# Row statistics of a layer norm taken from a router column and from ScalarE instead of VectorE

## The chip, the cores and the metric

The kernel runs on one core of a Trainium2 chip, as one launch. Its metric is the device time of that launch in microseconds (us). Three runs of the kernel before took 476.71, 476.83 and 477.4 us; the median is 476.83. A core has five engines with instruction lists of their own: TensorE (PE for matmuls, PEld for its weight loads), VectorE (DVE), ScalarE (ACT), GpSimd (POOL) and SyncE (SP, here only a queue that issues DMAs).

## The reference

The input x has 4096 tokens of 256 numbers. Two sublayers follow each other, each with a residual and a layer norm over the 256 numbers of a token:

```python
x = layernorm(x + mamba(x))        # y @ W_out is the last product of mamba; y has 512 numbers per token
x = layernorm(x + moe(x))          # each token goes to the one expert of 8 with the largest router logit

def layernorm(x, eps=1e-5):
    m = mean(x);  v = var(x)
    return (x - m) / sqrt(v + eps)
```

The mamba part is: a projection x @ W_in (256 to 1024 columns), a causal convolution over four tokens with SiLU, a small projection to one step size and 2 x 16 state numbers, a recurrence over the tokens with 16 states, a gate, and y @ W_out. The router's logits are `x1 @ Wr.T + br`, x1 being the output of the first layer norm. An expert is 256 to 1024 with ReLU and back to 256. Everything is float32.

## The kernel before, in words

The tokens go in eight blocks of 512 (NB = 8, TB = 512), and a block is four tiles of 128 tokens (JT = 4). The main loop (line 1047) runs eight rounds. Round k does the input projection of block k (`project`, eight column groups of 128), the small projection and the recurrence of block k-1 (`gauge`, `gauge_out`, `scan`), the gate, the output projection and the first layer norm of block k-2 (`gate`, `project_out`, `choose`), and the sorting of the tokens of block k-3 into lists by expert (`rank`, `place`, `blocks_of`, `tokens_of`). After some rounds blocks of 128 tokens of one expert are already sure, and quarters of their expert work (`expert`) are put between the pieces; most of it follows after the loop.

PE's order is the order in which the code is written (`manual_schedule` for PE, line 120). For DVE, ACT and POOL a scheduler orders the instructions when the kernel is built, from its own estimates and the order of the code; at run time each engine works through its list in that order. PSUM has eight banks: three for `mm` (products of `project` and of the experts), three for `o` (`gate`, `project_out`, the experts' second product) and two for `tr` (all else). A matmul into a bank waits until the bank's last reader is done.

The router is folded into the output projection. A layer norm subtracts the mean and divides by the standard deviation, so the logits are `(x + y W_out) @ Wr.T` with the mean taken out, times the inverse deviation, plus `br`. To that end `router_weights` (line 470) takes the mean over the 256 inputs out of the router's weights `wr`; `router_behind` (line 484) multiplies W_out by `wr` and puts the eight columns beside W_out, so `wout` is 256 + 8 columns wide; `look` (line 886) multiplies a block of x by `wr` (32 columns, of which eight are used), and `look_out` (line 901) turns this round, adds its two halves and writes the eight numbers of each token beside the token's x in `xb`, which is 256 + 8 wide as well.

`project_out(i, j)` (line 916) then multiplies tile j of the gated y (`sg`) by `wout` into a bank of 264 columns, and DVE adds that to `xb` (line 924): columns 0 to 255 hold x + y W_out, columns 256 to 263 the raw logits. DVE takes the row statistics with `bn_stats` (line 928) and `bn_aggr` (line 929). After the fourth tile ACT takes the square root of the four variances (line 934), DVE the reciprocal `sd` (line 935) and `nm`, minus mean times `sd` (line 937), and ACT writes the normed rows x1 (line 940), which SP's queue stores to `x1d` in DRAM (line 944). `choose` scales the raw logits with `sd`, adds `br` and picks the expert.

Other lines named below: ACT copies the products of `project` out of PSUM (lines 759, 761 and 763) and applies SiLU (line 772); DVE adds the convolution's taps (line 723); `gauge_out` makes the step sizes with an exponential on ACT (line 816) and a chain of small DVE steps; `scan` takes an exponential on ACT for `dA` (line 848), and on DVE `dBx` (line 850), the recurrence (line 852) and `hC` (line 860); `gate` sums `hC` over the states with a matmul into `py` (line 872), and DVE (line 879) and POOL or DVE (line 884) make `sg`. ACT loads a table of functions (rows named ACT_TABLE_LOAD) where the next function is not in the loaded one.

Of the kernel before, what the change touches and what calls it, by code (L numbers as in the profile page):

```python
# [37 lines left out]
F32 = mybir.dt.float32  # L38
# [3 lines left out]
AF = mybir.ActivationFunctionType  # L42
ALU = mybir.AluOpType
# [4 lines left out]
P = 128  # L48
T, D = 4096, 256
DI, NS, KC = 512, 16, 4  # L50
NE, FF = 8, 1024
TB = 512
NB = T // TB
JT = TB // P
NT = T // P
DC = D // P
CC = DI // P
# [26 lines left out]
OFF = 2 * NE * T  # L84
XW = 2 * NS + 1

O2 = DC * FF
OB = O2 + FC * D
OC = OB + FC
# [10 lines left out]
def mamba_moe(  # L100
# [17 lines left out]
    nc = tc.nc  # L118

    ctx.enter_context(tc.manual_schedule(engines={mybir.EngineType.PE}))  # L120
    const = ctx.enter_context(tc.tile_pool(name="const", bufs=1))
# [3 lines left out]
    a2 = ctx.enter_context(tc.tile_pool(name="a2", bufs=2))  # L125
    a3 = ctx.enter_context(tc.tile_pool(name="a3", bufs=3))

    def bank(tag, name, bufs=None):
        return ps.tile([P, 512], F32, tag=tag, name=name, bufs=bufs)
# [5 lines left out]
    st = {}  # L135

    def load(i):

        xTb = a2.tile([P, DC, TB], F32, tag="xTb", name=f"xTb{i}")
        at = slice(i * TB, (i + 1) * TB)  # L140
        if i:
            nc.sync.dma_start(xTb, xT[:, at].rearrange("(c p) t -> p c t", p=P))

        xb = a2.tile([P, JT, D + NE], F32, tag="xb", name=f"xb{i}")
        st[i] = {"xTb": xTb, "xb": xb}

    def load_rows(i):
        nc.sync.dma_start(
            st[i]["xb"][:, :, 0:D], x[i * TB : (i + 1) * TB, :].rearrange("(j p) d -> p j d", p=P)
        )  # L150

    load(0)


# [18 lines left out]

    wr = const.tile([P, DC, Q], F32, name="wr")
    nc.vector.memset(wr, 0.0)
    nc.sync.dma_start(wr[:, :, 0:NE], WrT.rearrange("(c p) e -> p c e", p=P))
    wx = const.tile([P, CC, H], F32, name="wx")
    nc.vector.memset(wx, 0.0)
    al = const.tile([NS, 1], F32, name="al")
    dp = const.tile([P, CC], F32, name="dp")  # L180

    wout = const.tile([P, CC, D + NE], F32, name="wout")
    brb = const.tile([P, NE], F32, name="brb")
    nega = const.tile([NS, 1], F32, name="nega")

# [10 lines left out]
    eps = const.tile([P, 1], F32, name="eps")  # L196
# [271 lines left out]
    woutT = held_weights[-1][:, 0 : DC * DI].rearrange("p (c n) -> p c n", c=DC)  # L468
# [14 lines left out]

    def router_behind(half):
        po = bank("tr", f"pwo{half}", 2)
        pov = po[:, 0 : CC * NE].rearrange("p (c e) -> p c e", e=NE)
        cs = slice(half * CC // 2, (half + 1) * CC // 2)
        for c in range(CC)[cs]:
            for dc in range(DC):
                nc.tensor.matmul(  # L490
                    pov[:, c, :], lhsT=woutT[:, dc, c * P : (c + 1) * P], rhs=wr[:, dc, 0:NE],
                    start=(dc == 0), stop=(dc == DC - 1),
                )
        nc.scalar.copy(wout[:, cs, D : D + NE], pov[:, cs, :])


    xgs, wes, turned, hid, last, open_, ys = {}, {}, {}, {}, {}, {}, {}
# [104 lines left out]
    def close(b, half):  # L602
# [5 lines left out]
        def out_weights(fc):  # L608
            return we[:, O2 + fc * D : O2 + (fc + 1) * D]

# [290 lines left out]
    def look_out(i):  # L901

        pf = bank("tr", f"pf{i}", 2)
        for s in range(2):
            at = slice(s * P, (s + 1) * P)
            nc.tensor.transpose(pf[:, at], st[i]["rx"][:, at], ident)

        pfv = pf[:, 0 : 2 * P].rearrange("p (s c h e) -> p s c h e", s=2, c=DC, h=2)
        beside = st[i]["xb"][:, :, D : D + NE].rearrange("p (h s) e -> p h s e", s=2)
        parts = a2.tile([P, 2, DC, 2, NE], F32, tag="rparts", name=f"rparts{i}", bufs=1)  # L910
        for s in range(2):
            nc.scalar.copy(parts[:, s], pfv[:, s, :, :, 0:NE])
        turned_parts = parts.rearrange("p s c h e -> p c h s e")
        nc.vector.tensor_tensor(beside, turned_parts[:, 0], turned_parts[:, 1], ALU.add)

    def project_out(i, j):
        s_, sg, xb = st[i], st[i]["sg"], st[i]["xb"]
        po = bank("o", f"po{i}_{j}")
        for c in range(CC):
            nc.tensor.matmul(  # L920
                po[:, 0 : D + NE], lhsT=sg[:, c, j * P : (j + 1) * P], rhs=wout[:, c, :],
                start=(c == 0), stop=(c == CC - 1),
            )
        nc.vector.tensor_tensor(xb[:, j, :], po[:, 0 : D + NE], xb[:, j, :], ALU.add)
        if j == 0:
            s_["mv"] = a2.tile([P, JT, 2], F32, tag="mva", name=f"mva{i}")
        sta = a2.tile([P, 6], F32, tag="sta", name=f"sta{i}_{j}")
        nc.vector.bn_stats(sta, xb[:, j, 0:D])
        nc.vector.bn_aggr(s_["mv"][:, j, :], sta)
        if j < JT - 1:  # L930
            return
        mv = s_["mv"]
        sd = s_["sd"] = a2.tile([P, JT], F32, tag="sda", name=f"sda{i}")
        nc.scalar.activation(sd, mv[:, :, 1], AF.Sqrt, bias=eps)
        nc.vector.reciprocal(sd, sd)
        nm = a2.tile([P, JT], F32, tag="nma", name=f"nma{i}")
        nc.vector.scalar_tensor_tensor(nm, mv[:, :, 0], -1.0, sd, ALU.mult, ALU.mult)
        x1 = a2.tile([P, JT, D], F32, tag="x1", name=f"x1{i}", bufs=1)
        for j in range(JT):
            nc.scalar.activation(  # L940
                x1[:, j, :], xb[:, j, 0:D], AF.Identity,
                scale=sd[:, j : j + 1], bias=nm[:, j : j + 1],
            )
        nc.sync.dma_start(
            x1d[i * TB : (i + 1) * TB, :].rearrange("(j p) d -> p j d", p=P), x1
        )
# [100 lines left out]
    for k in range(NB):  # L1047
        if have(k + 1):
            load(k + 1)
# [5 lines left out]
        a, b, c = k - 1, k - 2, k - 3  # L1055
# [3 lines left out]
        if k == 2:  # L1059
            router_behind(1)  # L1060
# [18 lines left out]
        if have(b):  # L1079
            project_out(b, 0)  # L1080
        expert(fill[3])
        project(k, 4)
        if k == 1:
            router_behind(0)
        if have(c):
            rank(c)
        if have(b):
            project_out(b, 1)
# [5 lines left out]
        if have(b):  # L1094
            project_out(b, 2)
        expert(fill[5])
        project(k, 6)
        if have(a):
            look_out(a)
            scan(a)  # L1100
# [11 lines left out]
    a, b, c = NB - 1, NB - 2, NB - 3  # L1112
# [12 lines left out]
    project_out(b, 2)  # L1125
    expert()
    look_out(a)
    scan(a)
    expert()
# [77 lines left out]
```

## Time and profile before

| | |
|---|---|
| runs, median | 476.71, 476.83, 477.4; 476.83 us |
| profiled execution: time, span | 479.7 us, 478.0 us |
| mean granted TensorE clock | 0.993 |
| PE busy | 466.2 us (98%) |
| DVE busy | 340.4 us (71%) |
| ACT busy | 223.4 us (47%) |
| POOL busy | 185.5 us (39%) |

The profile is of one execution; its span runs from the first to the last instruction, and 1.7 us of its time lie outside. Busy time leaves out waiting. Matmuls are pipelined and their ends are modelled, so a busy PE is not a PE at its peak. A group line gives line, engine, operation, result and operands with shapes, count, busy time, mean time of one, and after the second bar the idle time just before them with what ended it. A line of waits gives engine and line, what it waited for, the total, the number of times and the longest, in us.

### The profile page before, as it was taken

Reading aid. Unit: us, or ns where it says so; the run is one execution under the profiler, and the core shown is the slowest. Engines: PE = TensorE matmul, PEld = TensorE weight load, DVE = VectorE, ACT = ScalarE, POOL = GpSimd, SP = SyncE. Lnnn points to the kernel's source line nnn. Section 1 sums busy time; section 2 is a strip of 40 time slices with the busy share of each in tenths; the row PEclk is TensorE's granted clock in tenths of the full one; section 3 lists DMA queues with packets and bytes.
Section 4 is the critical chain, followed back from the end, with each engine's and each line's share of the span. In section 5 each row is a group of like instructions: output and inputs, shape, how many; then the busy total and the mean of one; then the engine's idle time right before and its main releaser. Section 6 shows DMA issues by size and latency. Waiting matters only on the chain. (4 is left out here: it accounts for less than half of the span.)

```text
span 478.0 us, 7559 instructions
## 1 busy us (share of the span) xinstructions
PE 466.2 (98%) x2606; PEld 350.1 (73%) x2606; DVE 340.4 (71%) x1120; ACT 223.4 (47%) x453; POOL 185.5 (39%) x194
## 2 busy tenths in 40 slices
PE   8999999999999999999999999999999999999994
PEld 6444554645455566677788999999989898989884
DVE  1687959899898997986998978755446565645453
ACT  3776767886896877584625131212212121212111
POOL 2001203442418372450433423435445456654541
PEclk9998999999999999999999999999999999999998
DMA  8401012040124945250766759799997279977910
GB/s 237 166 1 45 0 42 91 1 132 0 47 87 149 431 159 188 110 199 18 271 242 225 270 209 366 260 368 350 359 347 277 60 253 345 313 247 245 353 44 22
DMA packets 23401, 89.98 MB, mean 188 GB/s; under 512 B 4914, under 2 KB 14909, under 8 KB 19650
## 3 DMA queue, kind: packets, MB, share of 16 engines
q0 software_dynamic: 8752, 74.71, 42.7%
q1 hardware_dynamic: 13650, 14.50, 9.3%
q8 instruction: 21, 0.34, 0.3%
q10 hardware_dynamic: 960, 0.27, 0.3%
q14 instruction: 18, 0.15, 0.1%
HBM read 87.78 MB, written 9.43 MB: 203 GB/s over the span
## 5 line engine op out<-in xcount | busy, mean ns | idle before, releaser
L744 PE MATMUL pm<-xTb,win 128*128 128x512 f32 (+1 forms) x264 | 122.5, 598 | 0.0
L587 PEld LDWEIGHTS ph<-xgT,we 128*128 128x128 f32 x864 | 100.8, 192 | 5.5 <-DVE r L637 1.3
L587 PE MATMUL ph<-xgT,we 128*128 128x128 f32 x864 | 103.0, 276 | 0.0
L612 PE MATMUL pe<-we,hT 128*128 128x256 f32 x432 | 98.9, 380 | 0.0
L612 PEld LDWEIGHTS pe<-we,hT 128*128 128x128 f32 x432 | 79.7, 190 | 10.0 <-DVE lg L960 0.3
L723 DVE SCALAR_TENSOR_TENSOR acc<-xc,cw,acc 128x512 f32<-128x512 f32 x96 | 72.6, 777 | 15.7 <-DMA wx<-in_W_x 8.6
L744 PEld LDWEIGHTS pm<-xTb,win 128*128 128x128 f32 x264 | 49.2, 195 | 45.5 <-issue 40.8
L262 ACT ACTIVATE sdm<-mvm,eps 128x1 f32<-128x1 f32 x32 | 9.4, 294 | 122.6 <-DVE mvm L260 116.8
L522 POOL DMA_INDIRECT we<-in_experts,widx x32 | 33.6, 1049 | 85.0 <-DVE r L637 24.9
L920 PE MATMUL po<-wout,sg 128*128 128x264 f32 x256 | 64.1, 392 | 1.0 <-DVE sg L884 0.9
L884 POOL TENSOR_TENSOR sg<-cv,sg 128x512 f32<-128x512 f32 x22 | 32.7, 1492 | 59.6 <-DVE cv L879 46.1
L920 PEld LDWEIGHTS po<-wout,sg 128*128 128x128 f32 x256 | 46.1, 190 | 11.0 <-issue 2.9
L650 POOL DMA_INDIRECT out<-y,tidx x32 | 32.9, 1027 | 38.5 <-DVE y L264 30.5
L598 DVE TENSOR_SCALAR hT<-ph,we 128x128 f32<-128x128 f32 x108 | 31.3, 341 | 20.7 <-PE ph L587 20.6
L637 DVE TENSOR_TENSOR r<-pe,xs 128x256 f32<-128x256 f32 x32 | 13.5, 422 | 43.9 <-PE pe L612 43.8
L504 POOL DMA_INDIRECT xg<-x1d,tidx x32 | 31.9, 998 | 29.7 <-DVE xd L810 7.5
L596 ACT ACTIVATE hT<-ph,we 128x128 f32<-128x128 f32 x108 | 30.8, 368 | 23.2 <-PE ph L587 20.7
L1008 POOL TENSOR_SCALAR rowh<-lrow,row,code 128x256 f16<-128x256 bf16 x20 | 26.0, 1307 | 27.9 <-DVE row L1000 26.7
L879 DVE SCALAR_TENSOR_TENSOR cv<-cv,dp,py 128x256 f32<-128x256 f32 x64 | 28.5, 469 | 3.4 <-PE py L872 3.4
L759 ACT ACTIVATE sg<-pm 128x512 f32<-128x512 f32 x32 | 19.1, 596 | 19.5 <-PE pm L744 17.0
L761 ACT COPY xc<-pm 128x512 f32<-128x512 f32 x32 | 18.6, 582 | 19.1 <-PE pm L744 18.8
L763 ACT ACTIVATE acc<-pm,cb,cw 128x512 f32<-128x512 f32 x32 | 25.1, 784 | 0.0
(219 smaller groups left out, 604.4 us busy)
## 6 DMA issues: line engine op xcount, KB each, us to landing
xb<-in_x SPq DMA_DIRECT2D x8, 512.0 KB, 6.1
x1d<-x SPq DMA_DIRECT2D x8, 512.0 KB, 4.8
xTb<-in_xT SPq DMA_DIRECT2D x7, 512.0 KB, 3.3
win<-in_W_in SPq DMA_DIRECT2D x1, 512.0 KB, 5.2
we<-in_W_outT SPq DMA_DIRECT2D x1, 512.0 KB, 5.9
wout<-in_W_out SPq DMA_DIRECT2D x1, 512.0 KB, 6.9
we<-in_experts,widx POOLq DMA_INDIRECT x32, 10.3
xg<-x1d,tidx POOLq DMA_INDIRECT x32, 6.6
```

Source lines behind the costliest of these rows:

```text
L504: nc.gpsimd.indirect_dma_start(out=to, out_offset=None, in_=x1d[0:rows, :], in_offset=bass.IndirectOffsetOnAxis(ap=at, axis=0),)
L522: nc.gpsimd.indirect_dma_start(out=wes[n][:, :], out_offset=None, in_=experts, in_offset=bass.IndirectOffsetOnAxis(ap=weights[n], axis=0), ...
L587: nc.tensor.matmul(ph[:, n * w : (n + 1) * w], lhsT=we[:, at : at + P], rhs=xgT[:, dc * w : (dc + 1) * w], start=(dc == 0), stop=(dc == DC ...
L596: nc.scalar.activation(hT[:, fc, :], ph[:, n * w : (n + 1) * w], AF.Relu, bias=bias)
L598: last[b] = nc.vector.tensor_scalar(hT[:, fc, :], ph[:, n * w : (n + 1) * w], bias, 0.0, ALU.add, ALU.max)
L612: nc.tensor.matmul(py[:, 0:D], lhsT=hT[:, fc, 0:P], rhs=out_weights(fc), start=(fc == 0), stop=(fc == FC - 1),)
L650: moved = nc.gpsimd.indirect_dma_start(out=out, out_offset=bass.IndirectOffsetOnAxis(ap=at, axis=0), in_=rows, in_offset=None, bounds_chec ...
L723: nc.vector.scalar_tensor_tensor(acc, xc[:, c, k : k + TB], cw[:, c, k : k + 1], acc, ALU.mult, ALU.add)
L744: nc.tensor.matmul(banks[c][:, at], lhsT=win[:, dc, c * P : (c + 1) * P], rhs=xTb[:, dc, at], start=(dc == 0), stop=(dc == DC - 1),)
L879: nc.vector.scalar_tensor_tensor(cv[:, c, at], cv[:, c, at], dp[:, c : c + 1], py[:, 0 : TB // 2], ALU.mult, ALU.add,)
L884: eng.tensor_tensor(sg[:, c, :], cv[:, c, :], sg[:, c, :], ALU.mult)
L920: nc.tensor.matmul(po[:, 0 : D + NE], lhsT=sg[:, c, j * P : (j + 1) * P], rhs=wout[:, c, :], start=(c == 0), stop=(c == CC - 1),)
```

## The change

`wr` gets a ninth column of -1/256. The eight router columns have had their mean taken out; the ninth is left as it is. By the same way as the logits, through `look` and `look_out` for x and through `router_behind` and `wout` for y W_out, each token's row of `xb` then ends with minus its mean, in column 264. So `xb` and `wout` are 265 columns wide (D + NM), and so is the bank of `project_out`.

In place of `bn_stats` and `bn_aggr` on DVE, ACT computes Square of x + y W_out with that column as bias, and a row sum (`accum_out`); the squares themselves are not used. The square root takes the sum with a scale of 1/256. `nm` is the ninth column times `sd`.

```diff
+NM = NE + 1
@@ load
-        xb = a2.tile([P, JT, D + NE], F32, tag="xb", name=f"xb{i}")
+        xb = a2.tile([P, JT, D + NM], F32, tag="xb", name=f"xb{i}")
@@ weights
     nc.vector.memset(wr, 0.0)
+    nc.vector.memset(wr[:, :, NE:NM], -1.0 / D)
...
-    wout = const.tile([P, CC, D + NE], F32, name="wout")
+    wout = const.tile([P, CC, D + NM], F32, name="wout")
@@ router_behind
-                    pov[:, c, :], lhsT=woutT[:, dc, c * P : (c + 1) * P], rhs=wr[:, dc, 0:NE],
+                    pov[:, c, :], lhsT=woutT[:, dc, c * P : (c + 1) * P], rhs=wr[:, dc, 0:NM],
...
-        nc.scalar.copy(wout[:, cs, D : D + NE], pov[:, cs, :])
+        nc.scalar.copy(wout[:, cs, D : D + NM], pov[:, cs, :])
@@ look_out
-        beside = st[i]["xb"][:, :, D : D + NE].rearrange("p (h s) e -> p h s e", s=2)
-        parts = a2.tile([P, 2, DC, 2, NE], F32, tag="rparts", name=f"rparts{i}", bufs=1)
+        beside = st[i]["xb"][:, :, D : D + NM].rearrange("p (h s) e -> p h s e", s=2)
+        parts = a2.tile([P, 2, DC, 2, NM], F32, tag="rparts", name=f"rparts{i}", bufs=1)
         for s in range(2):
-            nc.scalar.copy(parts[:, s], pfv[:, s, :, :, 0:NE])
+            nc.scalar.copy(parts[:, s], pfv[:, s, :, :, 0:NM])
@@ project_out
-                po[:, 0 : D + NE], lhsT=sg[:, c, j * P : (j + 1) * P], rhs=wout[:, c, :],
+                po[:, 0 : D + NM], lhsT=sg[:, c, j * P : (j + 1) * P], rhs=wout[:, c, :],
                 start=(c == 0), stop=(c == CC - 1),
             )
-        nc.vector.tensor_tensor(xb[:, j, :], po[:, 0 : D + NE], xb[:, j, :], ALU.add)
+        nc.vector.tensor_tensor(xb[:, j, :], po[:, 0 : D + NM], xb[:, j, :], ALU.add)
         if j == 0:
-            s_["mv"] = a2.tile([P, JT, 2], F32, tag="mva", name=f"mva{i}")
-        sta = a2.tile([P, 6], F32, tag="sta", name=f"sta{i}_{j}")
-        nc.vector.bn_stats(sta, xb[:, j, 0:D])
-        nc.vector.bn_aggr(s_["mv"][:, j, :], sta)
+            s_["sq"] = a2.tile([P, JT], F32, tag="sqa", name=f"sqa{i}")
+        squares = a2.tile([P, D], F32, tag="sta", name=f"sta{i}_{j}")
+        nc.scalar.activation(
+            squares, xb[:, j, 0:D], AF.Square, bias=xb[:, j, D + NE : D + NM],
+            accum_out=s_["sq"][:, j : j + 1],
+        )
         if j < JT - 1:
             return
-        mv = s_["mv"]
         sd = s_["sd"] = a2.tile([P, JT], F32, tag="sda", name=f"sda{i}")
-        nc.scalar.activation(sd, mv[:, :, 1], AF.Sqrt, bias=eps)
+        nc.scalar.activation(sd, s_["sq"], AF.Sqrt, scale=1.0 / D, bias=eps)
         nc.vector.reciprocal(sd, sd)
         nm = a2.tile([P, JT], F32, tag="nma", name=f"nma{i}")
-        nc.vector.scalar_tensor_tensor(nm, mv[:, :, 0], -1.0, sd, ALU.mult, ALU.mult)
+        nc.vector.tensor_tensor(nm, xb[:, :, D + NE], sd, ALU.mult)
```

More of the change, by code (lines that the diff above doesn't have):

```diff
@@ L485, in router_behind @@
         po = bank("tr", f"pwo{half}", 2)
-        pov = po[:, 0 : CC * NE].rearrange("p (c e) -> p c e", e=NE)
+        pov = po[:, 0 : CC * NM].rearrange("p (c e) -> p c e", e=NM)
         cs = slice(half * CC // 2, (half + 1) * CC // 2)
```

## The prediction

> **What bounds the kernel now.** I read the page from the top: busy time, slices, the stretch table, and only then the waits of the engine that turned out to be full.
>
> ```profile
> PE 466.2 (98%) x2606; PEld 350.1 (73%) x2606; DVE 340.4 (71%) x1120; ACT 223.4 (47%) x453; POOL 185.5 (39%) x194
> PE   8999999999999999999999999999999999999994
> DVE  1687959899898997986998978755446565645453
> ACT  3776767886896877584625131212212121212111
> ```
>
> The second line onwards is the span in 40 slices, busy tenths. PE is at 9 in all but the first and the last slice, so the end is set by PE's list of matmuls plus whatever PE waits. The change works in the loop over token blocks, where DVE is at 8 to 9 and ACT at 6 to 8. The stretch table sharpens that (columns: stretch, its length, busy time of PE, PEld, DVE, ACT, POOL; two loop rounds of about 27 us, without expert work):
>
> ```profile
> 95.00:122.00 27.00, 26.05 (x107) 14.10 (x106) 24.48 (x71) 21.09 (x36) 10.52 (x8) 1.00 0.18 59
> 122.00:149.00 27.00, 26.57 (x109) 14.31 (x108) 25.45 (x92) 21.59 (x36) 10.87 (x9) 1.00 0.19 60
> ```
>
> DVE is busy 91 and 94% of a round, ACT 78 and 80%. What PE itself waits for between 30 and 300 us, which holds every place where the change acts, is this (engine, line, releaser: total us, times, longest):
>
> ```profile
> PE po L920 <- DVE sg L884: 0.9, 1, 0.9
> PE pt L846 <- ACT rx L899: 0.7, 1, 0.7
> PE pg L555 <- DMA xg<-x1d,tidx: 0.6, 1, 0.6
> PE prx L893 <- DVE rk L993: 0.4, 1, 0.4
> PE pxo L800 <- ACT codes L450: 0.3, 1, 0.3
> PE py L872 <- DVE hC L860: 0.2, 1, 0.2
> ```
>
> Together 3.1 us, of which DVE ends 1.5 us. That is the key reading: DVE is over 90% busy, and still PE loses only 1.5 us to it, 0.3% of the time. A lighter DVE cannot be worth much more. Relief on a nearly full engine pays only where the full engine is the last to arrive.
>
> **The change, part by part.** The sum stands against the profiled execution: span 478.0 us, 479.7 us in all, so 1.7 us lie outside the span. That is 2.9 us above the median of the runs shown (476.83); I add the sum to the median. The rows used are these (line, engine, shapes, count, busy us, mean ns):
>
> ```profile
> L928 DVE BATCH_NORM_STATS2 sta<-xb 128x6 f32<-128x256 f32 x32 | 13.4, 418 | 0.3
> L929 DVE BATCH_NORM_AGGREGATE mva<-sta 128x2 f32<-128x6 f32 x32 | 5.5, 173 | 0.5
> L937 DVE SCALAR_TENSOR_TENSOR nma<-mva,sda 128x4 f32<-128x4 f32 x8 | 3.8, 480 | 0.0
> L940 ACT ACTIVATE x<-xb,nma,sda 128x256 f32<-128x256 f32 x32 | 16.6, 590 | 6.8 <-DVE nma L937 6.8
> L920 PE MATMUL po<-wout,sg 128*128 128x264 f32 x256 | 64.1, 392 | 1.0 <-DVE sg L884 0.9
> ```
>
> *Removed from DVE:* 32 x (418 + 173 ns) = 18.9 us, or 2.4 us per round, which leaves DVE at about 22.1 of 27 us. The statement for nm (L937) becomes another form of the same size; its mean of 480 ns comes from a few long ones beside POOL's product (1.00 us at 127.06 and 154.16, POOL in L884 both times), and the new form meets the same company: counted at no change, between -2.6 us (eight at the 156 ns of L824, also 128x4) and +4.2 us (eight at 1.00 us) on DVE, hidden by the taps of L723 around it.
>
> *Added to ACT:* 32 Squares over 128x256 with a pointer bias, and the write of a row sum. No row has a row sum. Below: L596, one pointer, takes 368 ns at 128 columns and 401 at 176, 0.69 ns a column, so 456 ns at 256, with the sum free. Above: L940, the same size with two pointers, 590 ns, plus a whole small instruction for the sum, 206 ns (L816, 128x4): 796 ns. I take 590, the row of the same size. 32 x 590 = 18.9 us, 2.4 us per round: ACT goes to about 23.5 of 27 us, 87%. The work moves over at par.
>
> *Activation tables:* a load costs 1283 ns in every row here. Copy (L761, L809), Identity (L763, L940) and Relu (L596) have between them one load, at the start; Silu, Exp and Sqrt pay 48. I count Square among the former: zero loads. The other bound is one load in and one out for each Square, 64 x 1.283 = 82 us.
>
> A rule speaks against this. The Trainium skill, page "ScalarE: Activation LUTs", section "Table sets: the hidden batching unit", names relu, copy, identity and abs as fillers of every set, and not Square; read strictly, Square may force switches, which that page prices at about 2.66 us with the drain, an estimated 64 x 2.66 = 170 us. Its table of precision budgets does put square in one class with identity, relu and abs. No run here shows a Square yet.
>
> *The ninth column.* po goes from 264 to 265 columns in 256 matmul instructions. 64.1 us / (256 x 264) = 0.95 ns a column, times 256 = +0.24 us, on PE, not hidden. Above: L612 with 256 columns takes 98.9 / 432 = 229 ns each, L920 250 ns, so 2.7 ns a column and 0.7 us. Below: nothing, if PE is waiting there anyway. I take 0.24. The router product of a block (L893) already multiplies 32 columns, eight of them used; writing -1/256 into a ninth costs one more small memset on DVE, after the one of wr that took 112 ns at 0.9 us. The load of wr on SP's queue was issued at 4.30 us, so 3 us cover it. The 16 products of router_behind get one column, 16 x 0.95 ns; the copies of L494 and L912 and the additions of L914 and L924 one column in 8 or 264: under 0.1 us in all, off PE. Rows of xb and wout now begin every 1060 bytes instead of 1056. The load of xb lands in 6.1 us and is used two rounds (54 us) later; even doubled it is hidden. On SP's queue that load and the store of x1 wait for x1 (L940), which the paragraph on waits leaves where it was; POOL's queue is moved past nothing. For reading wout at such steps no row tells; bounded by the 2.7 ns a column above.
>
> *Waits.* The sum of squares now has to come from ACT before the square root, where DVE's aggregate did. So ACT has a new wait for DVE's addition (L924), four times a round; behind it in ACT's list stand the copies of rx and rparts, dA (L848), and the evictions of pm. Their cover: the pm banks. At 135.54 PE starts the product for column group 4 of block 5 in a bank that ACT's acc gave free at 131.32, 4.2 us earlier, the shortest distance of rounds 4 to 6; two Squares fit into it. Then the chain to py. ACT's and DVE's own rows in round 4:
>
> ```profile
> 116.32 0.36 ACT L899 COPY rx<-prx 128x256 f32<-128x256 f32 x1
> 118.81 0.60 ACT L759 ACTIVATE sg<-pm 128x512 f32<-128x512 f32 x1 [2.13 <-PE pm L744]
> 120.89 0.68 ACT L848 ACTIVATE dA<-pt,nega 16x512 f32<-16x512 f32 x1
> ...
> 121.25 0.43 DVE L924 TENSOR_TENSOR xb<-po,xb 128x264 f32<-128x264 f32 x1 [1.39 <-PE po L920]
> 121.72 0.68 DVE L850 TENSOR_TENSOR dBx<-pt,cv 16x512 f32<-16x512 f32 x1
> 122.33 0.41 DVE L928 BATCH_NORM_STATS2 sta<-xb 128x6 f32<-128x256 f32 x1
> 122.66 1.25 DVE L852 TENSOR_TENSOR_SCAN h<-dA,h,dBx 16x512 f32<-16x512 f32 x1
> 124.02 0.87 DVE L860 TENSOR_TENSOR hC<-pt,h 16x256 f32<-16x256 f32 x2
> ```
>
> ACT has 2.13 us of idle time just when the first two Squares are ready (their additions end by 115.3): they cost nothing. The third can delay dA, which ends at 121.57, by 0.6 us to 122.2; the scan needs dBx too, and that ends at 122.40. Without the statistics between dBx and the scan (0.41 and 0.14 us in the rows) hC is some 0.4 us earlier, so the delay is covered. The fourth shifts the square root (124.88) to about 125.8; the reciprocal that reads it ran at 126.60, behind the first products of py, so that is covered too. Next in line after a wait that goes is PE itself.
>
> *Sum on PE:* +0.24 (column); -0.4 for the wait on rk, since two statistics (0.41 + 0.17 us) go from DVE just ahead of it at 140.5 to 141.3; nothing for the wait of 0.9 us on sg, because between py and sg (97.9 to 108.3) DVE has no statistics, only the stretched small steps of choose, and it starts that stretch waiting for py. Total -0.2 us: **476.6 us**, no change that can be told. A measurement of this kernel can tell about 0.2%, 0.95 us. Own range of this case: 475.9 (both DVE waits lighter) to 478.2 (0.7 for the column and 0.7 from one late Square).
>
> **Rivals.** *Slower, ACT's order.* One Square is put ahead of rparts and dA and stands there until DVE's addition. DVE's addition itself waits up to 1.39 us for PE in the row above. Then dA slips by 0.59 + up to 1.4 us. It decides from a slip of about 1.2 us, that is 0.8 (dA at 121.57 to the end of dBx at 122.40) plus the 0.4 that the removed statistics give; beyond, hC is late, and hC now ends at 124.89, 0.2 us before py starts, so every further us stops PE. Price: a slip of 2.0 less 1.2, 0.8 us in each of rounds 2 to 5, 3.2 us: 476.6 + 3.2 = 479.8 us, range 478 to 481. For it: the cover of py is that thin in every round. Against: ACT has idle time in each round.
>
> *Faster, DVE was the last to arrive.* The whole 1.5 us of PE's waits for DVE go, the 0.6 us wait for a gathered row too because x1 is written earlier; less the column: 476.8 - 2.1 + 0.2 = 474.9 us, with half of it about 475.9; range 474.5 to 475.9. For it: DVE above 90%. Against: the longest of these waits lies where no statistic runs.
>
> *Square needs a table load.* 82 us on ACT; in the loop, 65 to 270 us, ACT is busy 141.6 of 205 us, so it would run over by 82 - 63 = 19 us: about 496 us.
>
> **How the numbers follow.** No visible change 0.42 (same 0.27, slower 0.09, faster 0.06); ACT's order 0.32, all slower; DVE relief 0.24, all faster; table loads 0.02. Hence faster 0.30, same 0.27, slower 0.43. The likeliest case gives 476.6 us. The range leaves out the loads, 0.08 of the slow case's upper end and 0.04 of the fast case's lower end: 474.8 to 480.3.
>
> **What would show it.** Right: no load rows at the Square's line; a Square at 0.5 to 0.8 us; DVE busy down by about 19 us and ACT up by as much; PE busy and the po spacing up by 0.2 us in total; PE's waits still near 3 us. Wrong: new waits of py (L872) or pt for hC or dA, evictions of pm more than 4 us late, Square with long idle time before it that DVE's addition ended. What would make it wrong above all is a different order on ACT and DVE over the whole loop, since a moved instruction can shift its neighbours; the trace of before cannot show that.

## The result and the profile after

The changed kernel takes 481.64 us (median of 10 runs, 480.38 to 484.65) beside 477.25 us for the kernel before on the same chip: a ratio of 1.0103, 95% interval 1.0074 to 1.0132. It is 1.0% slower, 4.4 us by the medians, and lies above the predicted range. The ratios here and below are taken over all runs of both kernels, so they differ a little from the quotient of the medians; one run of a later experiment that took 2754 us is left out of its ratio. In five of the thirteen profiles, that of the kernel before included, PE runs at half clock for 3.4 us at about 45 us (the row 45 to 46 us of the profile of before says 0.50), and executions with the lower granted clock that goes with it take some 2.3 us longer. So below matmuls are compared by their places, in profiles that are alike in this, and times of different chips only by their ratios.

The profiled execution took 481.92 us, with a span of 480.2 us. The lines of the changed kernel stand three further down than those of the kernel before (the copy of rx is L902), and four from the square root on (L938); the Square is L931.

The page of the changed kernel, busy time by engine:

```profile
PE 466.2 (97%) x2606; PEld 350.4 (73%) x2606; DVE 326.9 (68%) x1057; ACT 235.1 (49%) x513; POOL 185.6 (39%) x194
```

DVE has 13.5 us less than before, ACT 11.7 us more, and PE's busy time is the same to a tenth, while the span is 2.2 us longer than in the profile of before, which has that early half-clock window where this one has none. So the next view is what PE waits for. The changed kernel's waits of PE between 30 and 300 us:

```profile
PE pt L849 <- ACT rx L902: 3.6, 2, 2.9
PE py L875 <- DVE hC L863: 0.7, 2, 0.5
PE pg L558 <- ACT rparts L915: 0.5, 1, 0.5
PE pxo L803 <- ACT codes L453: 0.3, 1, 0.3
```

The two waits that DVE ended and that the prediction spoke of (on sg, 0.9, and on rk, 0.4) are gone from the list. In their place one wait for the copy of rx has grown from 0.7 to 3.6 us, 2.9 of it at once. The stretch table of the changed kernel (stretch, length, busy time of PE, PEld, DVE, ACT, POOL, then granted clock, DMA share, GB/s) finds the round:

```profile
95.00:122.00 27.00, 27.00 (x110) 14.46 (x108) 23.42 (x65) 22.98 (x43) 10.11 (x8) 1.00 0.20 65
122.00:149.00 27.00, 26.76 (x109) 14.46 (x108) 23.97 (x82) 21.54 (x43) 13.68 (x11) 1.00 0.25 77
149.00:176.00 27.00, 23.17 (x92) 12.86 (x92) 21.72 (x63) 19.63 (x39) 14.66 (x13) 0.97 0.77 302
```

The rounds at 95 and 122 us are better than before (PE 27.00 and 26.76 us busy, where it was 26.05 and 26.57). Most is lost in the next one, round 6. ACT's list there, by its timeline in the changed kernel (start, duration, line, operation; in brackets the idle time before and what ended it):

```profile
165.08 0.20 ACT L819 ACTIVATE e<-e 128x4 f32<-128x4 f32 x1
168.64 0.51 ACT L931 ACTIVATE sta<-xb 128x256 f32<-128x256 f32 x1 [3.35 <-DVE xb L927]
...
169.26 1.28 ACT L762 ACT_TABLE_LOAD   x1
170.55 0.60 ACT L762 ACTIVATE sg<-pm 128x512 f32<-128x512 f32 x1
...
171.57 0.50 ACT L931 ACTIVATE sta<-xb 128x256 f32<-128x256 f32 x1
...
173.05 0.37 ACT L902 COPY rx<-prx 128x256 f32<-128x256 f32 x1
```

The same stretch of ACT's list in the kernel before:

```profile
167.96 0.20 ACT L816 ACTIVATE e<-e 128x4 f32<-128x4 f32 x1
168.18 1.28 ACT L759 ACT_TABLE_LOAD   x1
169.48 0.60 ACT L759 ACTIVATE sg<-pm 128x512 f32<-128x512 f32 x1
...
171.49 0.37 ACT L899 COPY rx<-prx 128x256 f32<-128x256 f32 x1
```

Before, ACT goes on to the table load 0.02 us after e. Now the Square of tile 0 of block 4 stands between, and ACT is idle for 3.35 us in front of it, with the load, four Silus (L762 and L775, which are 759 and 772 before), the Square of tile 1 and the copy of rx queued behind. From the end of e to the start of rx it is 3.33 us before and 7.77 us after. What the Square waits for is DVE's addition of that tile. DVE's timeline in the changed kernel:

```profile
167.78 0.22 DVE L837 SCALAR_TENSOR_TENSOR sr<-q,delta 128x64 f32<-128x64 f32 x1
168.03 0.22 DVE L840 TENSOR_TENSOR sr<-xd,sr 128x64 f32<-128x64 f32 x1
168.18 0.43 DVE L927 TENSOR_TENSOR xb<-po,xb 128x265 f32<-128x265 f32 x1
```

The addition comes behind the whole chain of small steps that turns e into sr. It did so before too, but there only the bn statistics read it. And e, made by ACT, starts that chain: ACT hands DVE the work and then stands until DVE has done all of it and the addition.

The copy of rx empties a bank that pt's transposes need. PE's timeline in the changed kernel:

```profile
170.16 0.38 PE L909 MATMUL pf<-ident,rx 128*128 128x128 f32 x2
173.47 0.63 PE L849 MATMUL pt<-ident,sr 128*80 128x128 f32 x4 [2.93 <-ACT rx L902]
174.63 0.69 PE L558 MATMUL pg<-ident,xg 128*128 128x128 f32 x2 [0.52 <-ACT rparts L915]
175.11 3.17 PE L923 MATMUL po<-wout,sg 128*128 128x265 f32 x8
```

The same places in the kernel before:

```profile
172.71 0.60 PE L846 MATMUL pt<-ident,sr 128*80 128x128 f32 x4
...
174.18 1.95 PE L920 MATMUL po<-wout,sg 128*128 128x264 f32 x8
```

PE stops for 2.93 us. The eight products of po behind the stall then take 3.17 us, where eight took 1.95 us before. The first of them start 441 instead of 223 ns apart, and the granted clock, the third number from the end in the changed kernel's stretch table, shows why:

```profile
172.00:174.00 2.00, 0.53 (x4) 0.37 (x4) 0.00 (x0) 2.00 (x8) 2.00 (x3) 1.00 0.00 0
174.00:176.00 2.00, 1.48 (x6) 1.16 (x5) 0.62 (x2) 1.97 (x5) 0.96 (x1) 0.54 0.00 0
176.00:178.00 2.00, 2.00 (x7) 1.61 (x6) 0.68 (x1) 0.57 (x1) 0.00 (x0) 0.61 0.00 0
```

From 174.2 to 177.6 us PE has half its clock, which by the matmuls' places costs another 1.3 to 1.6 us.

Set against a kernel with the ninth column but with the statistics still on DVE (the first experiment, without the early half-clock window, as here), the n-th matmul of the changed kernel is earlier by 0.29, 0.34, 0.28 and 0.31 us at about 70, 105, 132 and 138 us, sum 1.2 us gained; then later by 0.91 us at py of round 5, by 3.23 us at pt of round 6, and by 1.55 us over the half clock, sum 5.7 us lost. That makes +4.5 us, and the spans are 475.8 and 480.2 us.

### The profile page after: what moved, and what is told of

It reads as the page before. It is cut to its first block, busy times and chain, and to the rows that moved or that the text cites. A ratio compares the mean times of both kernels' runs of the same rounds, so it can differ in the third digit from the quotient of the medians.

```text
span 480.2 us, 7575 instructions
## 1 busy us (share of the span) xinstructions
PE 466.2 (97%) x2606; PEld 350.4 (73%) x2606; DVE 326.9 (68%) x1057; ACT 235.1 (49%) x513; POOL 185.6 (39%) x194
## 4 chain that ended last, share of the span: by engine, by line
PE 84%; DVE 7%; ACT 3%; issue 3%; DMA 1%; POOL 0%; POOLq 0%; SPq 0%; ACTq 0%
PE ph L590 24%; PE pe L615 22%; PE pm L747 18%; PE po L923 11%; PE px L790 3%; DVE acc L726 2%; PE pg L558 2%; PE pf L626 1%; PE py L875 1%; DMA win<-in_W_in 1%; DVE h L855 1%; PE prx L896 1%; DVE cv L882 1%; ACT sg L762 1%; PE pxo L803 1%
## 5 line engine op out<-in xcount | busy, mean ns | idle before, releaser
L747 PE MATMUL pm<-xTb,win 128*128 128x512 f32 (+1 forms) x264 | 121.1, 591 | 0.3 <-DMA win<-in_W_in 0.3
L726 DVE SCALAR_TENSOR_TENSOR acc<-xc,cw,acc 128x512 f32<-128x512 f32 x96 | 73.6, 797 | 15.4 <-DMA wx<-in_W_x 8.8
L923 PE MATMUL po<-wout,sg 128*128 128x265 f32 x256 | 65.2, 397 | 0.0
L923 PEld LDWEIGHTS po<-wout,sg 128*128 128x128 f32 x256 | 47.2, 194 | 10.1 <-issue 3.0
L887 POOL TENSOR_TENSOR sg<-cv,sg 128x512 f32<-128x512 f32 x22 | 30.5, 1399 | 60.9 <-DVE cv L882 59.3
L640 DVE TENSOR_TENSOR r<-pe,xs 128x256 f32<-128x256 f32 x32 | 13.5, 423 | 45.3 <-PE pe L615 45.3
L931 ACT ACTIVATE sta<-xb 128x256 f32<-128x256 f32 x32 | 16.2, 507 | 31.7 <-DVE xb L927 27.2
L775 ACT ACTIVATE cv<-acc 128x512 f32<-128x512 f32 x32 | 20.1, 628 | 10.3 <-DVE acc L726 10.3
```

The lines of the kernel that those rows point to most:

```text
L726: nc.vector.scalar_tensor_tensor(acc, xc[:, c, k : k + TB], cw[:, c, k : k + 1], acc, ALU.mult, ALU.add)
L747: nc.tensor.matmul(banks[c][:, at], lhsT=win[:, dc, c * P : (c + 1) * P], rhs=xTb[:, dc, at], start=(dc == 0), stop=(dc == DC - 1),)
L887: eng.tensor_tensor(sg[:, c, :], cv[:, c, :], sg[:, c, :], ALU.mult)
L923: nc.tensor.matmul(po[:, 0 : D + NM], lhsT=sg[:, c, j * P : (j + 1) * P], rhs=wout[:, c, :], start=(c == 0), stop=(c == CC - 1),)
```

## The experiments

The line numbers in the fences are those of each kernel. The theory: Squares that stand in ACT's list ahead of copies on which PE depends cost the time, by their waiting and not by their duration. The rivals: the ninth column; too much work on ACT wherever it stands; and, for what was gained, an accident of order and not the lighter DVE.

### The column alone

The ninth column stays; variance and nm are taken from bn statistics on DVE as before.

```diff
-        squares = a2.tile([P, D], F32, tag="sta", name=f"sta{i}_{j}")
-        nc.scalar.activation(
-            squares, xb[:, j, 0:D], AF.Square, bias=xb[:, j, D + NE : D + NM],
-            accum_out=s_["sq"][:, j : j + 1],
-        )
+        sta = a2.tile([P, 6], F32, tag="sta", name=f"sta{i}_{j}")
+        nc.vector.bn_stats(sta, xb[:, j, 0:D])
+        nc.vector.bn_aggr(s_["mv"][:, j, :], sta)
```

> The ninth column and its copies stay, the row statistics are back on DVE; the lists of all engines have the order of the kernel before. Theory of the waiting Square: the column costs 256 x 0.95 ns = 0.24 us and nothing else, so about 477.5 us against 477.25 before; no wait of PE for the copy of rx in round 6. Rival, the column itself costs the time (unaligned rows, 265 columns): most of the +4.4 us is here, 480 to 482 us, with the spacing of the po matmuls up by several ns.

477.38 us, ratio 1.001 (0.9989 to 1.0031). The column costs too little to show in the time, and the loss lies with the Squares and the order that came with them. By the starts of the matmuls, the products of po are 225 instead of 223 ns apart, some 0.5 us over 256 of them. One more thing shows in it. The order of the lists is that of the kernel before (but for one pair of small steps on DVE at 90 us and the memset at the start), and yet the wait on sg at 107 us is not there. A step of choose on DVE, ahead of that sg, is the difference; the kernel before and then this one, each by DVE's timeline:

```profile
104.78 1.30 DVE L968 TENSOR_TENSOR oh<-back,best 128x32 bf16<-128x32 f32 x1
```

```profile
103.46 0.18 DVE L971 TENSOR_TENSOR oh<-back,best 128x32 bf16<-128x32 f32 x1
```

The same instruction takes 1.30 or 0.18 us. The wait on sg that the prediction read from one profile was partly a matter of which small step met a slow moment in that execution.

### Two tiles back on DVE

The Squares of tiles 0 and 1 of block 4, which stand in front of rx in round 6, go back to DVE as bn statistics; the other 30 stay.

```diff
+        if i == NB - 4 and j < 2:
...
+            nc.vector.bn_stats(sta, xb[:, j, 0:D])
...
+            nc.vector.bn_aggr(mv1, sta)
+            nc.vector.tensor_scalar(s_["sq"][:, j : j + 1], mv1[:, 1:2], float(D), None, ALU.mult)
+        else:
...
+            nc.scalar.activation(
+                squares, xb[:, j, 0:D], AF.Square, bias=xb[:, j, D + NE : D + NM],
+                accum_out=s_["sq"][:, j : j + 1],
+            )
```

> The changed kernel, but tiles 0 and 1 of block 4 get their variance from DVE again; 30 of 32 Squares stay, and the other lists keep their order. Theory of the waiting Square: PE's wait for rx (2.9 us) and the half-clock stretch after it (about 1.7 us) go, 481.6 - 4.6 = 477.0 us (476 to 478). Rival, ACT carries too much work in general: two of 32 Squares are 0.3 us, so 481 us or more.

480.69 us, ratio 1.0072 (1.004 to 1.0104): a miss. The stall at pt went as expected, but its like came up one place further, and the loss at py of round 5 (about 1 us) stayed. ACT and PE in the timeline of this kernel:

```profile
170.10 0.37 ACT L902 COPY rx<-prx 128x256 f32<-128x256 f32 x1
...
174.07 0.51 ACT L938 ACTIVATE sta<-xb 128x256 f32<-128x256 f32 x1 [3.60 <-DVE xb L927]
...
175.06 0.27 ACT L915 COPY rparts<-pf 128x36 f32<-128x36 f32 x2
...
175.38 0.44 PE L558 MATMUL pg<-ident,xg 128*128 128x128 f32 x2 [2.91 <-ACT rparts L915]
```

rx is on time; now the Square of tile 2 is the first, its addition on DVE is behind the statistics that were put back, and it stands 3.60 us in front of rparts, for which pg's transposes wait. The step that failed in the expectation was that tile 2 had its addition by then. The mechanism holds, its place depends on which Square is first in the list.

### Two Squares later, in block 4 alone

All 32 Squares stay on ACT. Those of tiles 0 and 1 of block 4 are issued behind the copy of rx of the round (`copied[i + 2]`), with the one of tile 2 next; DVE's list is that of the changed kernel.

```diff
+        if i == NB - 4:
+            if j == 2:
+                with tc.issue_after(copied[i + 2].ins):
+                    for n in range(3):
+                        square(n)
+            elif j > 2:
+                square(j)
+        else:
+            square(j)
```

> The changed kernel with the same work, all 32 Squares on ACT; in ACT's list alone the Squares of tiles 0 and 1 of block 4 stand behind the copy of rx instead of ahead of it. Theory of the waiting Square: 477.0 us (476 to 478), PE's wait for rx gone. Rival, too much work on ACT: no change, 481.6 us.

479.62 us, ratio 1.0028 (1.0004 to 1.0051): above the 476 to 478 that were expected, and below the rival's 481.6. PE's waits in this kernel, 30 to 300 us:

```profile
PE pg L558 <- ACT rparts L917: 1.4, 1, 1.4
PE py L875 <- DVE hC L863: 0.7, 2, 0.5
PE pt L849 <- ACT rx L904: 0.7, 1, 0.7
```

The place of two Squares in ACT's list alone gives back some three quarters of the loss: pt waits 0.7 us as before the change, and the half clock behind it is gone. The work on ACT is the same, so its amount was not the cause of that part. Three Squares now stand ahead of rparts, one of which waits 1.13 us, and 1.4 us at pg are new.

### One Square more in the kernel before

The opposite test: the kernel before with one Square and its row sum, whose result nobody uses, right behind e of round 6 (`grown_[i + 1]`). DVE's list is unchanged.

```diff
+        if (i, j) == (NB - 4, 0):
+            extra = a2.tile([P, D + 1], F32, tag="extra", name="extra", bufs=1)
+            with tc.issue_after(grown_[i + 1].ins):
+                nc.scalar.activation(
+                    extra[:, 0:D], xb[:, j, 0:D], AF.Square, bias=eps,
+                    accum_out=extra[:, D : D + 1],
+                )
```

> The kernel before with one instruction more: a Square with a row sum over tile 0 of block 4, not used by anything, in ACT's list right behind the exponential of round 6, as in the changed kernel. Nothing else differs. Theory of the waiting Square: it stands there until DVE has added the tile, rx comes late, PE waits 2 to 3 us and then runs at half clock for a while: 477.25 + 3.0 to 4.7 = 480.3 to 482 us. Rival, work on ACT: +0.5 us of ACT work that is covered, 477.3 us.

482.23 us, ratio 1.0075 (1.0047 to 1.0103). ACT and PE in its timeline:

```profile
170.49 0.51 ACT L934 ACTIVATE extra<-xb,eps 128x256 f32<-128x256 f32 x1 [2.99 <-DVE xb L926]
...
174.40 0.37 ACT L901 COPY rx<-prx 128x256 f32<-128x256 f32 x1
...
174.82 1.02 PE L848 MATMUL pt<-ident,sr 128*80 128x128 f32 x4 [2.63 <-ACT rx L901]
```

An instruction of 0.51 us costs more than 3 us. It waits 2.99 us for the addition, and pt, which already runs at half clock here (1.02 instead of 0.60 us), comes 2.63 us late. One of the 32 Squares is enough for most of the loss (1.0075 of 1.0103), and nothing else of the change is needed for it.

### PE kept at work in the stall

The changed kernel with 13 transposes of the identity, whose results nobody uses, between pf and pt of round 6.

```diff
+        if i == NB - 3:
+            for n in range(13):
+                at = slice((2 + n % 2) * P, (3 + n % 2) * P)
+                nc.tensor.transpose(pf[:, at], ident, ident)
```

> The changed kernel with 13 unused transposes of the identity, 128 columns each, put into PE's list between the transposes of pf (L909) and pt (L849) of round 6, so that PE has something to execute while it would stand at pt. Idle cause: the half clock at 174.2 to 177.6 us of the changed kernel follows the stall because PE executed almost nothing for 3 us before it; with the gap partly filled the products of po behind it keep their 223 ns spacing, and the 1.3 to 1.7 us that the half clock cost come back while the 2.9 us of the stall stay: about 480.0 us, no 0.5 row at that place, and a granted clock of the whole span at 0.997 or 0.993 instead of 0.994 or 0.990. Rival, load cause: the clock falls there because of the dense work before it, and filling changes nothing or adds to it: 481.6 us or more, with the same half-clock window at 174 us. In both, the Square of tile 0 still stands some 3.3 us for DVE's addition.

This ran on another chip, where the kernel before takes 485.78 us (480.6 to 489.09). The four kernels profiled there show waits of PE in the experts' products that the profiles of the other chips don't have, 1.8 to 2.6 us at 417 to 421 us and 0.9 to 1.3 us at 463 to 468. They are taken here for waits for expert weights, but the profile names no releaser for the first of them, and there is no profile of the kernel before from that chip. The times there are read as ratios. This one: 1.0053 (1.0021 to 1.0085), against 1.0103 and 1.0113 for the changed kernel on two other chips. The intervals overlap, so the trace has to decide. The stretch table of this kernel:

```profile
172.00:174.00 2.00, 0.63 (x4) 0.37 (x4) 0.00 (x0) 2.00 (x8) 2.00 (x3) 1.00 0.00 0
174.00:176.00 2.00, 1.90 (x10) 1.66 (x11) 0.62 (x2) 1.97 (x3) 0.42 (x1) 1.00 0.00 0
176.00:178.00 2.00, 2.00 (x19) 1.97 (x18) 1.90 (x3) 0.71 (x4) 0.00 (x0) 1.00 0.00 0
```

The Square still waits (3.35 us), PE's filler (1.58 us) and what is left of its wait (1.51 us) make the same stall, and the clock stays at 1.00: eight products of po take 1.96 us instead of 3.17. That is what the idle cause expected, but this run alone does not prove it, since not every such stall is followed by half clock: with two tiles back on DVE PE stood 2.91 us and kept its clock. The Trainium skill, page "TensorE: Matmul & The Clock Gate", section "What's actually happening", says that the clock is halved after an idle window of about 3.4 us of a counter that runs freely. The traces fit that, and they show where the windows lie. The granted clock changes only on a grid of 3.413 us: in the kernel with one Square more at 45.22, 48.63, 174.92 and 178.34 us, whose distances are 1, 37 and 1 such windows. Here are the windows around the stall on the grid of the changed kernel's own trace, then those of the kernel with two tiles back, then those of the filled stall:

```profile
170.74:174.15 3.41, 0.63 (x4) 0.37 (x4) 0.18 (x1) 3.41 (x10) 3.41 (x4) 1.00 0.02 9
174.15:177.56 3.41, 2.93 (x8) 2.41 (x9) 1.30 (x3) 2.39 (x5) 0.81 (x1) 0.50 0.00 0
```

```profile
170.87:174.29 3.42, 1.60 (x9) 0.81 (x7) 2.93 (x12) 0.22 (x1) 2.19 (x2) 1.00 0.19 65
174.29:177.70 3.41, 2.32 (x13) 2.04 (x14) 0.97 (x3) 3.00 (x7) 2.91 (x3) 1.00 0.00 0
```

```profile
168.64:172.06 3.42, 2.79 (x18) 1.89 (x16) 1.68 (x6) 3.39 (x8) 2.82 (x4) 1.00 0.22 70
172.06:175.47 3.41, 2.00 (x11) 1.60 (x12) 0.62 (x2) 3.38 (x10) 2.36 (x2) 1.00 0.00 0
```

The stall of the changed kernel fills most of one window, which leaves PE 0.63 us busy; the stall of 2.91 us lies across a boundary at 174.29, and neither window falls below 1.60. In all thirteen profiles a window of the grid with PE busy for 0.95 us or less is followed by half clock, and one with 1.60 us or more is not, but for the one at about 45 us. What lies between 0.95 and 1.60 no run here shows. So it is PE's standing still that brings the half clock at 174 us, and not the work before it. The filled stall lies across a boundary too: without the filler its first window would have had some 1.4 us, in the gap that no run covers, so whether the filler or the place of the stall kept the clock there stays open.

### The root first

The kernel before, with ACT's square root issued ahead of the Silu of column group 7, where the changed kernel has it. The statistics stay on DVE.

```diff
-            evicted = nc.scalar.activation(sg[:, c - CC, :], pm, AF.Silu)
+            with tc.issue_after(rooted[i - 2].ins) if c == 7 and i - 2 in rooted else ExitStack():
+                evicted = nc.scalar.activation(sg[:, c - CC, :], pm, AF.Silu)
```

> The kernel before, with one thing moved: ACT's square root (sda) is issued ahead of the Silu of column group 7 instead of behind it; all statistics stay on DVE. Root theory: what took away PE's wait of 1.1 us on sg at 107 us and the 0.2 us at 134 us in the changed kernel was not the lighter DVE but this earlier root, behind which DVE's reciprocal, nm and choose steps run before the products of py instead of beside the gate. Then the wait on sg goes here as well and the time is 1.0 to 1.5 us under the kernel before of the same clock, about 475.7 us. Rival, load theory: the lighter DVE removed it; then the wait on sg stays near 0.9 us and the time is that of the kernel before, 477.0. If the root ahead costs an additional table load a round (1.28 us on ACT), the evictions behind it are late, and the time rises by up to 1 us.

Ratio 0.9995 (0.9962 to 1.0028), on the chip of the filled stall; the interval is too wide to tell the two theories apart by the time. PE's waits in this kernel, 30 to 300 us:

```profile
PE prx L894 <- DVE rk L994: 1.5, 1, 1.5
PE pt L847 <- ACT rx L900: 0.7, 1, 0.7
```

The wait on sg has gone with the order alone, 1.2 us by the place of the matmuls, so the lighter DVE was not needed for that. But the wait for rk grew from 0.4 to 1.5 us, 1.1 us given back a round later, behind a stretch of DVE's list that still holds the statistics. The order moves the waits of DVE about; in the runs here both are gone only where DVE has less work.

### Squares behind rx and behind dA

The changed kernel, Squares 0 and 1 behind the copy of rx (`copied`), 2 and 3 behind dA (`decayed`); first in block 4 alone, then in every block of the loop.

```diff
+            if j == 2:
+                with tc.issue_after(copied[i + 2].ins):
+                    for n in range(2):
+                        square(n)
+            elif j > 2:
+                with tc.issue_after(decayed[i + 1].ins):
+                    for n in (2, 3):
+                        square(n)
```

> The changed kernel with only ACT's order altered in round 6: the Squares of tiles 0 and 1 of block 4 behind the copy of rx, those of tiles 2 and 3 behind dA; DVE's list is that of the changed kernel. Theory of the waiting Square: no waiting Square then stands ahead of rx, rparts or dA, the stalls at pt (2.9 us) and at pg (1.4 us with three Squares behind rx) both fall to the 0.6 to 0.8 us of the kernel before, and the half clock after them goes. From 481.6: less 3.1 (pt), less 1.3 to 1.7 (half clock), less about 0.3 (early half-clock window, present in some executions): about 476.7 us, and 476.3 at the higher granted clock; the 0.7 us at py of round 5 stay. Rival, load theory (ACT simply has too much to do, wherever the Squares stand): 480 us or more.

> The same order (Squares 0 and 1 behind rx, 2 and 3 behind dA) in every block of the loop, not in block 4 alone. Theory of the waiting Square: the 0.7 us at py of round 5, where the Square of tile 2 stands 1.55 us ahead of rparts and dA, go too, and what the lighter DVE gains (1.1 us on sg, 0.3 on rk, 0.3 on sg of the next round) is all that is left: 475.5 us, 474.8 to 476.4, under the kernel before. Rival: the Squares put behind dA make the square root late, and with it nm, x1 and the gathers, by 1 us or more in the other rounds: 477.5 to 479 us, with a new wait on sg or on the gathered rows.

On the chip with the longer waits in the experts' products the first gave 0.9973 (0.9941 to 1.0005) and the second 0.9928 (0.9893 to 0.9963). In the first, the matmuls after pt are 2.9 us earlier than in the changed kernel and the half clock behind is gone, pg waits 0.9 us. In the second, the 0.5 us at py of round 5 are gone as well: hC ends 0.2 us of PE's time in all, as in the kernel before. The second order once more, on a chip without those waits, together with the changed kernel:

> The changed kernel itself once more, on the same chip as the two orders beside it, so that the three can be set against each other and against the kernel before. Expected: 1.0% over the kernel before (0.7 to 1.3%), with the Square of tile 0 of block 4 standing about 3.3 us and PE about 2.9 us behind it at pt, then a half-clock window of 3.4 us.

> Squares 0 and 1 behind rx, 2 and 3 behind dA, in every block of the loop, a second time, beside the changed kernel on one chip. Waiting-Square theory: 4.5 to 5.5 us under the changed kernel and 1.0 to 1.9 us (0.2 to 0.4%) under the kernel before, the PE matmuls of the loop's end about 1.3 us earlier than with the statistics on DVE and the column alone. Rival, that the gain of the first run of this order came from the waits for expert weights of that chip: equal to the kernel before within 0.2%.

The kernel before took 477.36 us there. The changed kernel: 483.87 us, 1.0113 (1.0074 to 1.0151), with the same stall of 2.9 us at pt. The order in every block: 476.1 us, 0.9977 (0.9954 to 0.9999), which is 1.4% (6.5 us) under the changed kernel, more than the 4.5 to 5.5 us expected. The loss is gone. Against the kernel before the gain is 0.2%, by an interval that ends just under 1; the next order settles it better. That the gain was 0.7% on the other chip speaks for the rival there, that most of it came from the waits in the experts' products; without a profile of the kernel before from that chip this stays open.

### One Square behind rx, three behind dA

Against the kernel of the experiment before this one:

```diff
-                    for n in range(2):
-                        square(n)
+                    square(0)
...
-                    for n in (2, 3):
+                    for n in range(1, JT):
                         square(n)
```

> Only the Square of tile 0 behind rx, those of tiles 1, 2 and 3 behind dA, in every block of the loop. In the order before this one the Square of tile 1 still stood 1.1 to 1.4 us ahead of rparts in round 6 and PE waited 0.85 us at pg. Theory: that falls to 0.3 us or less, as rparts then follows the copy of rx and one Silu; three Squares behind dA take 1.5 us there and end before the fourth's addition, so the square root stays where it was: 0.4 to 0.6 us under the order with two ahead, about 0.5% under the kernel before. Rival: rparts was late for another reason (the transposes of pf, or the Silu and its table load ahead of it), and nothing changes; or the three Squares make the square root late, and the time rises by up to 1 us.

476.46 us, 0.9974 (0.995 to 0.9997), on the chip of the pair above. PE's waits, 30 to 300 us:

```profile
PE pt L851 <- ACT rx L904: 0.7, 1, 0.7
PE pxo L803 <- ACT codes L453: 0.3, 1, 0.3
PE pg L558 <- ACT rparts L917: 0.2, 1, 0.2
PE py L877 <- DVE hC L865: 0.2, 1, 0.2
```

The wait at pg fell from 0.9 to 0.2 us, and the matmuls behind it are 0.66 us earlier than with two Squares ahead. As a time it can't be told from that order. It can be told from the kernel before: the six executions with a granted clock of 0.996 or more (474.55 to 475.60 us) all lie below the fastest of the 23 of the kernel before on that chip (475.93), and the other six (477.32 to 477.65) below all of its executions of a lower clock (478.39 and more). PE loses 1.4 us between 30 and 300 us now, 3.1 in the kernel before, and DVE ends 0.2 us of it, so a lighter DVE has little more to give.

## Why the prediction was wrong, point by point

**What bounds the kernel: right.** PE's list plus PE's waits set the end in every run, and "Relief on a nearly full engine pays only where the full engine is the last to arrive" is what was measured: 13.5 us less on DVE went with 1.2 us gained in the changed kernel, beside its losses, and with about 1.7 us less waiting (the 3.1 less 1.4 above) in the best order, of which the 0.9 us on sg also go without a lighter DVE.

**Removed from DVE, the table loads and the ninth column: right in the main.** The 18.9 us of statistics are gone, nm went from 480 to 160 ns each, to the lower end of what was named. The page's busy times moved by less than the 19 us named as a sign of being right (DVE 13.5, ACT 11.7): the page counts time that two neighbouring instructions share once (the durations of DVE's instructions, added up, fell by 18.9 us), and ACT has four table loads of 1.28 us less. The Square has no load row; there are 45 loads in all instead of 49, so the strict reading of the Trainium skill, page "ScalarE: Activation LUTs", section "Table sets: the hidden batching unit", by which Square would not be a filler of every set, does not hold here. The column took about 0.5 us of PE by the spacing of po, between the 0.24 taken and the 0.7 named as the upper bound.

**The duration of a Square: right in size, not in form.** The changed kernel's groups, each form apart:

```profile
L931 ACT ACTIVATE sta<-xb 128x256 f32<-128x256 f32 x32 | 16.2, 507 | 31.7 <-DVE xb L927 27.2 <-DVE row L409 4.2
L931 ACT ACTIVATION_READ_ACCUMULATOR sta<-xb 128x1 f32 x32 | 6.0, 188 | 0.0
```

507 ns and a row of its own for the sum, 188 ns, together 695 between the bounds of 456 and 796; 590 was taken. The same line holds the miss: the Squares are busy for 16.2 us and ACT stands idle in front of them for 31.7. Most of that idle time costs nothing: 20.3 us of it are still there in the best order. What costs is where it lies.

**The waits: wrong, and here is the step.** The prediction saw the new wait ("So ACT has a new wait for DVE's addition (L924), four times a round; behind it in ACT's list stand the copies of rx and rparts, dA (L848)"), and then costed it from the rows of round 4: "ACT has 2.13 us of idle time just when the first two Squares are ready (their additions end by 115.3): they cost nothing." In round 4 the addition comes early on DVE. In round 6 it comes behind the chain from e to sr, and the profile of before had that: e ends on ACT at 168.16 us and the addition on DVE starts 2.5 us later, with rx not yet copied (its copy starts at 171.49):

```profile
170.69 0.42 DVE L924 TENSOR_TENSOR xb<-po,xb 128x264 f32<-128x264 f32 x1
```

A Square right behind e in that round had to stand until that addition's end, some 3 us; the one Square more showed 2.99. One round was taken for all. What the profile of before could not show is that the Square would be put right there; the prediction named such a new order as its main risk ("since a moved instruction can shift its neighbours"), and its likeliest case put no price on it.

**The slower rival: right mechanism, wrong place and price.** It had the Square standing until DVE's addition, "ahead of rparts and dA", in rounds 2 to 5, through hC to py, at 0.8 us a round, 479.8 us. That path cost 0.9 us, in round 5 only. The rest came through rx and the bank of pt, a path that the prediction named only as something behind the wait: its cover was looked for in the banks of pm, 4.2 us, while rx was 0.85 us ahead of pt in round 6 of the kernel before (it ends at 171.86, pt starts at 172.71), and PE already waited 0.7 us for it in round 1 (at 38 us). And a stall was priced at its own length; 1.3 to 1.6 us of half clock came on top. So the term of 3.2 us (four rounds of 0.8) measured 0.9 at py, 3.2 at pt and 1.5 of clock, with 1.2 gained elsewhere. That its 479.8 us came within 2 us of the measured time is in part luck.

**The wait on sg: wrong.** "Nothing for the wait of 0.9 us on sg" was argued from DVE having no statistics there. In the changed kernel it is gone. The earlier root on ACT takes it away by itself, and so does a small step that happens to be short. The wait for rk fell from 0.41 to 0.09 us, by 0.3 where 0.4 was expected.

**The faster rival** was right that DVE was the last to arrive at sg, rk and py; it needs an order on ACT in which the Squares stand behind what PE waits for.

## What to carry to other kernels

When work is moved to an engine that works through a fixed list, price the wait and not the duration: for each round by itself, take the end of the operand's producer, the instruction ahead, and everything queued behind up to the first thing that the bounding engine needs. The worst case is an operand whose producer itself waits for the instruction just ahead in the same list. If the sum on the moved engine looks harmless and the kernel is slower, change the place of the moved instructions alone before giving the change up: here 1.0% slower became 0.2 to 0.3% faster by order.

## What was not expected of the hardware

A stall of PE can cost half as much again: three of the four stalls of 2.6 to 2.9 us in round 6 that were looked at ended in 3.4 us of half clock. Whether one does depends on where it falls on the grid of 3.413 us, and a window of that grid need not be idle throughout: those with PE busy for 0.49 to 0.95 us were followed by half clock, those with 1.60 us and more (but for the one below) were not. The half-clock window at about 45 us is another matter. By the granted clocks it comes in some executions of the same kernel and not in others, and those with the lower clock take some 2.3 us longer (before, on two chips: medians 476.4 to 476.7 us at a granted clock of 0.996 and more, 478.8 to 479.0 below). Half the clock for 3.4 us takes at most 1.7 us of that. PE is busy for 1.8 of the 2.0 us before it and for 3.2 us of the window of the grid. What brings it stays open.

A row sum on ACT has an instruction of its own, the read of 188 ns, and is still no second pass: Squares whose operands are ready follow each other, read included, every 0.49 us (171.31 and 171.80 us in the last order). The normed rows (L944 in the changed kernel), of the same size and without a sum, also start every 0.49 us, at 590 ns each.
